# A selective scan that multiplies by C from SBUF: VectorE's products of two banks joined into one

## The chip, the cores and the metric

The kernel runs on one core of a Trainium2 chip. What is measured is the device time of one execution, in microseconds. Three runs of the kernel before took 8867.66, 8870.62 and 8871.87 us; their median, 8870.62, is the time before.

A core has five engines that work side by side and wait for each other through semaphores: PE (TensorE, matrix products into PSUM), ACT (ScalarE, functions and copies), DVE (VectorE), POOL (GpSimd) and SP, which issues DMA transfers. Each takes its instructions in a fixed order. SBUF and PSUM are the two memories on the chip[...].

## The reference

Four layers follow each other on four images of 64 x 64 tokens with 128 channels, all in fp32: a visual state-space block, an attention over all tokens of an image, a convolution block, and a neighbourhood attention with an MLP. The change lies in the first, whose core is a scan in four directions over the 4096 tokens of an image, with 256 channels (d) and 16 states (n) each:

```python
def step(h, t):
    x_t, d_t, B_t, C_t = t
    h = jnp.exp(d_t[..., None] * A) * h + (d_t * x_t)[..., None] * B_t[:, :, None, :]
    return (h, jnp.einsum('bkdn,bkn->bkd', h, C_t))
scan_in = (jnp.moveaxis(xs, -1, 0), jnp.moveaxis(delta, -1, 0), jnp.moveaxis(Bs, -1, 0), jnp.moveaxis(Cs, -1, 0))
h0 = jnp.zeros((Bn, K, DI, N), input.dtype)
_, ys_l = jax.lax.scan(step, h0, scan_in)
```

So for each channel and state: a factor exp(delta A), an input delta x B, the recurrence, a product with C, and a sum over the states.

## The kernel before

`network` (L1654 and below) first prepares image 0's scan inputs (`scan_inputs`: layer norm, projection, convolution, delta, and du = delta x) and then, at a lower urgency, emits the scans of all four images. Beside image 0's scan it emits the inputs of images 1 to 3, beside the scan of image `img` the remaining layers of image `img - 1` (`rest`), and after the last scan the remaining layers of image 3. A scheduler lays out each engine's instructions from priorities, so the scan's instructions and the other layers' are interleaved in each engine's fixed order.

`selective_scan` (L454 to L578) goes through four directions `k`, eight chunks of 512 tokens, two halves `hf` of the channels, four groups `j` of four states, and two pairs `pp`. One turn of the innermost loop is a *unit*: 128 partitions are 32 channels by 4 states, and two groups `g` of channels lie beside each other, so a unit is 128 x 2 x 512. There are 4 x 4 x 8 x 2 x 4 x 2 = 2048 units. Each does:

- POOL: `dB` = du x B, both in SBUF, 128 x 1024 (L501). `dB` has four tiles.
- ACT: `dA` = exp(delta A) into a PSUM bank, once for each `g` (L507). `dA` has three banks.
- DVE: the recurrence along 512 tokens, once for each `g` (L509), with dA, dB and the state that the chunk before left.
- the product with C, into a tile `hc`, by one of two engines. `ON_POOL` says by which, by the unit's number modulo 16: 5 of 16 units in image 0 and 7 of 16 in the others are POOL's, 832 in all; 1216 are VectorE's.
- PE: the sum over the states by a product with a matrix of zeros and ones, into `py` (L555).

In a unit whose product is POOL's, the scans write `hc` in SBUF, and POOL multiplies `hc` by `c_rows` in place, 128 x 1024 (L522); this instruction is put behind the dB of `BEHIND` = 2 later units. The last states of both `g` go to `state` in one copy by ACT (L518). In a unit whose product is VectorE's, a scan writes over `dA` in its PSUM bank, VectorE multiplies that bank by `c_rows` into a half of `hc` (L514, 128 x 512, once for each `g`), and ACT copies the last state out of the bank (L516), again once for each `g`. In all chunks but the last of a direction the state is kept.

A `dB` tile comes free when the unit's scans are done, a `dA` bank when its product and state copy are done. `Products` gives the `hc` tiles; `b_rows`, `c_rows`, `dt` and `du` come by DMA from DRAM, issued by SP.

`scan_inputs` has a tile `sz` for silu(z), 128 x 2 x 512, in a pool of two buffers (L351); ACT fills it (L359) and a DMA in ACT's queue stores it (L382) once for each of the 32 chunks. `scan_output` builds a small matrix `center` on VectorE from two SBUF tiles (L601), once for each image.

Of the kernel before, what the change touches and what calls it, by code (L numbers as in the profile page):

```python
# [28 lines left out]
F32 = mybir.dt.float32  # L29
# [10 lines left out]
ND = DI // 128  # L40
FF = 4 * C
NF = FF // 128
LC = 512
NCH = NT // LC
# [19 lines left out]
def bc(ap, shape):  # L64
    return ap.to_broadcast(list(shape))


def mid(ap, n):

    return bc(ap.unsqueeze(1), [ap.shape[0], n, ap.shape[1]])  # L70


def span(c, n=LC):
    return slice(c * n, (c + 1) * n)
# [103 lines left out]
def layernorm_T(tc, K, pool, psum, x, w, b, out):  # L178


    nc = tc.nc
    stats = pool.tile([128, 4, 6], F32, name="ln_stats", bufs=2)
    mv = pool.tile([128, 4, 2], F32, name="ln_mv", bufs=2)
    rstd = pool.tile([128, 4], F32, name="ln_rstd", bufs=2)
    less = pool.tile([128, 4], F32, name="ln_less", bufs=2)
    shift = pool.tile([128, 4], F32, name="ln_shift", bufs=2)
    for t in range(4):
        nc.vector.bn_stats(stats[:, t, :], x[:, t, :])
    for t in range(4):
        nc.vector.bn_aggr(mv[:, t, :], stats[:, t, :])  # L190
    rstd_of(nc, K, rstd, mv[:, :, 1])
    nc.scalar.activation(less, rstd, AF.Copy, scale=-1.0)
    for t in range(4):
        nc.scalar.activation(shift[:, t : t + 1], mv[:, t, 0:1], AF.Copy, scale=less[:, t : t + 1])
    xn = pool.tile([128, 4, 128], F32, name="ln_xn", bufs=1)
    pt = psum.tile([128, 4, 128], F32, name="ps")
    for t in range(4):
        nc.scalar.activation(  # L198
            xn[:, t, :], x[:, t, :], AF.Identity, bias=shift[:, t : t + 1], scale=rstd[:, t : t + 1]
        )  # L200
        nc.tensor.transpose(pt[:, t, :], xn[:, t, :], K.ident)  # L201
    nc.scalar.activation(out, pt.rearrange("p t c -> p (t c)"), AF.Identity, bias=b, scale=w)  # L202
# [37 lines left out]
def conv3x3(nc, out, lhsT, src, row0, nrows, height):  # L240


    taps = [(0, 0)] + [(dy, dx) for dy in (-1, 0, 1) for dx in (-1, 0, 1) if (dy, dx) != (0, 0)]
    for i, (dy, dx) in enumerate(taps):
        r0, r1 = max(row0, -dy), min(row0 + nrows, height - dy)
        c0, c1 = max(0, -dx), min(W, W - dx)
        mm = nc.tensor.matmul(  # L247
            out[:, r0 - row0 : r1 - row0, c0:c1],
            lhsT((dy + 1) * 3 + dx + 1),
            src[:, r0 + dy : r1 + dy, c0 + dx : c1 + dx],  # L250
            start=(i == 0),
            stop=(i == len(taps) - 1),
        )
    return mm


def token_tiles(dram, c):

    return dram[span(c), :].rearrange("(t p) c -> p t c", p=128)
# [17 lines left out]
def scan_inputs(tc, K, A, D, img):  # L277
# [4 lines left out]
    nc = tc.nc  # L282
    with ExitStack() as ctx:
        pool = ctx.enter_context(tc.tile_pool(name="si_a", bufs=2))
# [49 lines left out]
        for c in range(NCH + 1):  # L334
            acts = []
            if c < NCH:
                xt = pool.tile([128, 4, 128], F32, name="x")
                nc.sync.dma_start(xt, token_tiles(A["x"][img], c))
                xnT = pool.tile([128, LC], F32, name="xnT")
                layernorm_T(tc, K, pool, psum, xt, ln_w, ln_b, xnT)  # L340
                band = pool.tile([128, ND, RC + 2, W], F32, name="band", bufs=3)
                bands[c] = band
                for d in range(ND):
                    ps = psum.tile([128, LC], F32, name="ps")
                    nc.tensor.matmul(ps, in_proj[:, d * 128 : (d + 1) * 128], xnT, start=True, stop=True)
                    rows = ps.rearrange("p (h w) -> p h w", w=W)
                    nc.scalar.copy(band[:, d, 1 : RC + 1, :], rows)
                    if c > 0:
                        nc.scalar.copy(bands[c - 1][:, d, RC + 1, :], rows[:, 0, :])
                        nc.scalar.copy(band[:, d, 0, :], bands[c - 1][:, d, RC, :])  # L350
                sz = pool.tile([128, ND, LC], F32, name="sz")  # L351
                for d in range(ND):
                    ps = psum.tile([128, LC], F32, name="ps")
                    mm = nc.tensor.matmul(
                        ps, in_proj[:, DI + d * 128 : DI + (d + 1) * 128], xnT, start=True, stop=True
                    )
                    if d == 0:
                        together.open(mm)
                    acts.append(lambda d=d, ps=ps, sz=sz: nc.scalar.activation(sz[:, d, :], ps, AF.Silu))  # L359
            if c > 0:  # L360

                b, src = c - 1, bands.pop(c - 1)
                top, bottom = (1 if b == 0 else 0), (RC + 1 if b == NCH - 1 else RC + 2)
                for d in range(ND):
                    ps = psum.tile([128, LC], F32, name="ps")
                    mm = conv3x3(
                        nc,
                        ps.rearrange("p (h w) -> p h w", w=W),
                        lambda t, d=d: diag[:, d, t, :],
                        src[:, d, top:bottom, :],  # L370
                        1 - top,
                        RC,
                        bottom - top,
                    )
                    acts.append(
                        lambda d=d, ps=ps, b=b: nc.scalar.activation(
                            xc[:, d, span(b)], ps, AF.Silu, bias=conv_b[:, d : d + 1]
                        )
                    )
            together.run(mm, acts)  # L380
            if c < NCH:
                nc.scalar.dma_start(D.sz[img][c], sz)  # L382
            if c > 0:
                nc.scalar.dma_start(D.xc[img][c - 1], xc[:, :, span(c - 1)])
                steps(0, c - 1)
# [68 lines left out]
def selective_scan(tc, K, S, D, img):  # L454
# [8 lines left out]
    nc = tc.nc  # L463
    pool, psum, products = S.pool, S.psum, S.products
    waiting = []

    def settle(unit):
        while waiting and waiting[0][0] <= unit:
            waiting.pop(0)[1]()

    for k in ORDER:
        back = k >= 2
        order = slice(None, None, -1) if back else slice(None)
        last = 0 if back else LC - 1
        state = pool.tile([128, NJS, NPR, 2], F32, name="state")
        for i in range(NCH):
            c = NCH - 1 - i if back else i
            for hf in range(2):
# [11 lines left out]
                for j in range(NJS):  # L490

                    bt, ct = (pool.tile([128, LC], F32, name=name, bufs=4) for name in ("b_rows", "c_rows"))
# [4 lines left out]
                    hcs, made = [], []  # L497
                    for pp in range(2):
                        pr = 2 * hf + pp
                        dB = pool.tile([128, 2, LC], F32, name="dB", bufs=4)  # L500
                        nc.gpsimd.tensor_mul(dB, dus[pp], mid(bt, 2))  # L501
                        on_pool = S.unit % 16 in ON_POOL[img > 0]
                        S.unit += 1
                        hc = products.tile()
                        for g in range(2):
                            dA = psum.tile([128, LC], F32, name="dA", bufs=3)
                            nc.scalar.activation(dA, dts[pp][:, g, :], AF.Exp, scale=S.A[:, k, j, pr, g : g + 1])  # L507
                            hg = hc[:, g, :] if on_pool else dA
                            nc.vector.tensor_tensor_scan(  # L509
                                hg[:, order], dA[:, order], dB[:, g, order],  # L510
                                0.0 if i == 0 else state[:, j, pr, g : g + 1], ALU.mult, ALU.add,
                            )
                            if not on_pool:
                                mm = nc.vector.tensor_mul(hc[:, g, :], dA, ct)  # L514
                                if i < NCH - 1:
                                    nc.scalar.copy(state[:, j, pr, g : g + 1], dA[:, last : last + 1])  # L516
                        if on_pool and i < NCH - 1:
                            nc.scalar.copy(state[:, j, pr, :], hc[:, :, last])  # L518
                        if on_pool:

                            def product(hc=hc, ct=ct, made=made):
                                made.append(nc.gpsimd.tensor_mul(hc, hc, mid(ct, 2)))  # L522

                            waiting.append((S.unit + BEHIND, product))
                        else:
                            made.append(mm)
                        hcs.append(hc)
                        settle(S.unit)
# [1260 lines left out]
```

## Time and profile before

| what | value |
|---|---|
| median of three runs | 8870.62 us |
| the profiled execution's own time | 8860.92 us |
| its span | 8859.2 us |
| granted TensorE clock, mean | 0.861 |
| instructions | 102397 |
| units, with product on POOL / on VectorE | 832 / 1216 |

The last columns of a group's row in the profile are: busy time of the group in us, mean ns of one, then the idle time of its engine just before the instructions of the group, and what ended most of that. A group is named by its line, engine and operation, then what it writes, an arrow, and what it reads, by the names of the tiles. Instructions of an engine overlap at their ends, so two that follow each other take a little less than twice the length of one.

### The profile page before, as it was taken

The numbers are of one execution on the slowest core, as the hardware profiler recorded it, in microseconds if no ns is written. First come the engines' busy times: TensorE is split into PE (matmuls) and PEld (weight loads), VectorE is DVE, ScalarE is ACT, GpSimd is POOL, SyncE is SP. The second block draws the span as 40 slices with busy tenths as digits, with TensorE's granted clock in tenths as the row PEclk, the third lists the DMA queues.
The fourth block names the chain that finished last, engine by engine and source line by source line (L and its number), as shares of the span: only waits on it lengthen the run. The fifth ranks groups of instructions, "written<-read, shape, count | busy, mean of one in ns | idle before, by whom it ended". The sixth has DMA issues, their size and how long they took to land. (4 is left out here: it accounts for less than half of the span.)

```text
span 8859.2 us, 102397 instructions
## 1 busy us (share of the span) xinstructions
PE 7107.5 (80%) x30596; PEld 2643.4 (30%) x30596; DVE 7138.3 (81%) x8531; ACT 5683.3 (64%) x11661; POOL 7046.2 (80%) x3079
## 2 busy tenths in 40 slices
PE   6845858686788888887798988887899888888987
PEld 2211213132332222333322222333322223343333
DVE  4888978787999999998899999998899999313433
ACT  5646767676666676667766676667766766354365
POOL 6988999989899999998899989998899989300000
PEclk8756868687899998887899988888899988899989
DMA  5777776777555556666445556565445565220021
GB/s 183 246 233 247 244 254 233 265 241 257 188 169 168 173 166 218 193 214 194 164 167 173 175 187 216 193 218 182 159 165 180 179 211 194 77 70 4 1 82 30
DMA packets 863923, 1576.24 MB, mean 178 GB/s; under 512 B 218597, under 2 KB 345212, under 8 KB 859645
## 3 DMA queue, kind: packets, MB, share of 16 engines
q1 hardware_dynamic: 733053, 1393.40, 47.8%
q10 hardware_dynamic: 130304, 176.19, 5.6%
q8 instruction: 245, 4.01, 0.2%
q14 instruction: 321, 2.63, 0.1%
HBM read 1276.02 MB, written 282.28 MB: 176 GB/s over the span
## 5 line engine op out<-in xcount | busy, mean ns | idle before, releaser
L501 POOL TENSOR_TENSOR dB<-du,b_rows 128x1024 f32<-128x1024 f32 x2048 | 4808.9, 2378 | 451.2 <-issue 136.8
L507 ACT ACTIVATE dA<-dt,w_A_log 128x512 f32<-128x512 f32 x4096 | 2782.9, 691 | 482.0 <-DVE hc L509 213.5
L509 DVE TENSOR_TENSOR_SCAN dA<-dA,state,dB 128x512 f32<-128x512 f32 x2128 | 2630.0, 1272 | 277.1 <-POOL dB L501 138.8
L522 POOL TENSOR_TENSOR hc<-hc,c_rows 128x1024 f32<-128x1024 f32 x832 | 1979.2, 2379 | 54.3 <-issue 21.3
L509 DVE TENSOR_TENSOR_SCAN hc<-dA,state,dB 128x512 f32<-128x512 f32 x1456 | 1801.9, 1267 | 171.1 <-ACT dA L507 100.0
L514 DVE TENSOR_TENSOR hc<-dA,c_rows 128x512 f32<-128x512 f32 x2432 | 1564.6, 675 | 74.8 <-PE py L555 60.5
L555 PE MATMUL py<-hc,pick 128*32 128x512 f32 x8192 | 1254.7, 690 | 377.6 <-POOL hc L522 277.9
L516 ACT COPY state<-dA 128x1 f32<-128x1 f32 x2128 | 327.2, 159 | 1329.9 <-DVE hc L514 1320.7
L845 PE MATMUL pa<-e,l_v 128*128 128x512 f32 x2048 | 1056.5, 647 | 19.8 <-ACT e L801 19.7
L797 PE MATMUL pair<-l_g,l_f 32*128 32x512 f32 x2048 | 529.5, 665 | 176.7 <-ACT e L801 121.7
L985 POOL MEMSET l_h<- 64x128 f32 x8 | 1.7, 211 | 837.2 <-DVE l_h L959 834.9
L801 ACT ACTIVATE e<-pair 128x1024 f32<-128x1024 f32 (+1 forms) x448 | 508.3, 1135 | 219.2 <-PE pair L797 211.1
L845 PEld LDWEIGHTS pa<-e,l_v 128*128 128x128 f32 x2048 | 373.9, 199 | 672.1 <-issue 615.8
L555 PEld LDWEIGHTS py<-hc,pick 128*32 128x32 f32 x8192 | 209.2, 116 | 1156.8 <-issue 458.6
L247 PE MATMUL ps<-band,w_conv_diag 128*128 128x504 f32 (+3 forms) x1152 | 498.2, 592 | 6.1 <-ACT delta L397 5.7
L1317 PE MATMUL pair<-table,ident 128*128 128x512 f32 x768 | 404.4, 652 | 101.8 <-ACT e L1327 80.6
L509 DVE TENSOR_TENSOR_SCAN dA<-dA,dB 128x512 f32<-128x512 f32 x304 | 356.0, 1212 | 64.5 <-POOL dB L501 51.7
L1327 ACT ACTIVATE e<-pair 128x1024 f32<-128x1024 f32 (+1 forms) x224 | 254.9, 1138 | 192.6 <-PE pair L1321 192.0
L328 POOL TENSOR_TENSOR du<-delta,xc 128x1024 f32<-128x1024 f32 x128 | 332.9, 2607 | 52.2 <-ACT delta L397 46.7
L201 PE MATMUL ps<-ident,ln_xn 128*128 128x128 f32 x512 | 137.3, 367 | 257.8 <-ACT ln_xn L198 185.0
L219 PE MATMUL ps<-xnT,w_fc_w 128*128 128x512 f32 x512 | 270.2, 662 | 69.9 <-ACT xnT L202 29.2
L247 PEld LDWEIGHTS ps<-band,w_conv_diag 128*128 128x128 f32 x1152 | 220.4, 192 | 283.2 <-issue 262.5
(276 smaller groups left out, 8680.4 us busy)
## 6 DMA issues: line engine op xcount, KB each, us to landing
b_rows<-bc_dram SPq DMA_DIRECT2D x1024, 256.0 KB
c_rows<-bc_dram SPq DMA_DIRECT2D x1024, 256.0 KB
dt<-delta_dram SPq DMA_DIRECT2D x512, 512.0 KB
du<-du_dram SPq DMA_DIRECT2D x512, 512.0 KB
delta_dram<-delta ACTq DMA_DIRECT2D x128, 512.0 KB
du_dram<-du SPq DMA_DIRECT2D x128, 512.0 KB
table<-biasT_dram SPq DMA_DIRECT2D x72, 512.0 KB
y_first_dram<-y_sum ACTq DMA_DIRECT2D x128, 256.0 KB
```

Of the source, the lines that this page charges most:

```text
L247: mm = nc.tensor.matmul(out[:, r0 - row0 : r1 - row0, c0:c1], lhsT((dy + 1) * 3 + dx + 1), src[:, r0 + dy : r1 + dy, c0 + dx : c1 + dx], s ...
L328: nc.gpsimd.tensor_mul(du.rearrange("p d (a b) -> p d a b", b=H), deltas[b].rearrange("p d (a b) -> p d a b", b=H), tk,)
L501: nc.gpsimd.tensor_mul(dB, dus[pp], mid(bt, 2))
L507: nc.scalar.activation(dA, dts[pp][:, g, :], AF.Exp, scale=S.A[:, k, j, pr, g : g + 1])
L509: nc.vector.tensor_tensor_scan(hg[:, order], dA[:, order], dB[:, g, order], 0.0 if i == 0 else state[:, j, pr, g : g + 1], ALU.mult, ALU.add,)
L514: mm = nc.vector.tensor_mul(hc[:, g, :], dA, ct)
L522: made.append(nc.gpsimd.tensor_mul(hc, hc, mid(ct, 2)))
L555: mm = nc.tensor.matmul(py[0][32 * q : 32 * q + 32, :], S.pick, hcs[q // 2][:, q % 2, :], start=(k == 1 and j == 0), stop=(j == NJS - 1),)
L797: nc.tensor.matmul(ps[:, u, :], f[quad, t // 4, span(t % 4, 128)], g[quad, c, :], start=True, stop=True)
L801: made = nc.scalar.activation(e, ps, AF.Exp)
L845: nc.tensor.matmul(pa, v[:, 8 * q + t, :], es[q], start=(t == 0 and q == 0), stop=(t == 7 and q == 3),)
L1317: nc.tensor.matmul(ps[:, u, :], K.ident, t[:, u, :], start=True, stop=False)
```

## The change

In a unit whose product is VectorE's, the scan of each `g` now writes over its half of `dB` in SBUF, not over `dA` in PSUM. When both scans are done, one VectorE instruction multiplies all 1024 columns of `dB` by `c_rows` (taken twice) into `hc`, and ACT copies both last states in one instruction. The `dA` bank comes free with the scan; the `dB` tile comes free with the product and the state copy. `dB` has a fifth tile, and `sz` has one buffer instead of two. Units whose product is POOL's do what they did. The lines behind the change move up by two: POOL's product is L520, PE's sum L553, and both kinds of state copy are L516.

```diff
-                sz = pool.tile([128, ND, LC], F32, name="sz")
+                sz = pool.tile([128, ND, LC], F32, name="sz", bufs=1)
...
-                        dB = pool.tile([128, 2, LC], F32, name="dB", bufs=4)
+                        dB = pool.tile([128, 2, LC], F32, name="dB", bufs=5)
                         nc.gpsimd.tensor_mul(dB, dus[pp], mid(bt, 2))
...
                             nc.scalar.activation(dA, dts[pp][:, g, :], AF.Exp, scale=S.A[:, k, j, pr, g : g + 1])
-                            hg = hc[:, g, :] if on_pool else dA
+                            hg = (hc if on_pool else dB)[:, g, :]
                             nc.vector.tensor_tensor_scan(
                                 hg[:, order], dA[:, order], dB[:, g, order],
                                 0.0 if i == 0 else state[:, j, pr, g : g + 1], ALU.mult, ALU.add,
                             )
-                            if not on_pool:
-                                mm = nc.vector.tensor_mul(hc[:, g, :], dA, ct)
-                                if i < NCH - 1:
-                                    nc.scalar.copy(state[:, j, pr, g : g + 1], dA[:, last : last + 1])
-                        if on_pool and i < NCH - 1:
-                            nc.scalar.copy(state[:, j, pr, :], hc[:, :, last])
+                        if not on_pool:
+                            mm = nc.vector.tensor_mul(hc, dB, mid(ct, 2))
+                        if i < NCH - 1:
+                            nc.scalar.copy(state[:, j, pr, :], (hc if on_pool else dB)[:, :, last])
```

## Prediction

> **What bounds the kernel now.** I read the busy shares of the page first, then its slices, then one undisturbed stretch of the scan.
>
> ```profile
> PE 7107.5 (80%) x30596; PEld 2643.4 (30%) x30596; DVE 7138.3 (81%) x8531; ACT 5683.3 (64%) x11661; POOL 7046.2 (80%) x3079
> ...
> DVE  4888978787999999998899999998899999313433
> ...
> POOL 6988999989899999998899989998899989300000
> ```
>
> Three engines stand at about 80%, which says little. The slices say more: POOL works in eights and nines into slice 35 and then stops. That is the end of the scan; the last VectorE product of the timeline ends at 7618 us. So the span is 7618 us of scan, with other layers beside it, and 1241 us of the last image's later layers, which the change doesn't touch. In the table by stretch the line 2600 to 3200 holds scan and attention; its columns are the stretch, its length, and busy time (instructions) of PE, PEld, DVE, ACT, POOL, then clock, DMA share, GB/s.
>
> ```profile
> 2600.00:3200.00 600.00, 536.45 (x2210) 159.29 (x2210) 566.48 (x608) 398.25 (x753) 600.00 (x260) 0.95 0.52 171
> ```
>
> POOL is busy 600.00 of 600 us here: it is the bound, with DVE 5% behind. The groups give the prices.
>
> ```profile
> L501 POOL TENSOR_TENSOR dB<-du,b_rows 128x1024 f32<-128x1024 f32 x2048 | 4808.9, 2378 | 451.2 <-issue 136.8
> L509 DVE TENSOR_TENSOR_SCAN dA<-dA,state,dB 128x512 f32<-128x512 f32 x2128 | 2630.0, 1272 | 277.1 <-POOL dB L501 138.8
> L514 DVE TENSOR_TENSOR hc<-dA,c_rows 128x512 f32<-128x512 f32 x2432 | 1564.6, 675 | 74.8 <-PE py L555 60.5
> L854 DVE TENSOR_TENSOR total<-total,e 128x2048 f32<-128x2048 f32 x56 | 128.3, 2292 | 136.9 <-ACT e L801 136.8
> L601 DVE TENSOR_TENSOR center<-center,ident 128x128 f32<-128x128 f32 x4 | 15.9, 3984 | 0.1
> ```
>
> The last row is the one to stop at. L601 adds two 128x128 tiles that both lie in SBUF; its four durations are 11.21, 0.28, 4.15 and 0.29 us. The two short ones ran while POOL did nothing. The timeline (start, length, engine) shows what the long ones had beside them:
>
> ```profile
> 2214.86 6.93 POOL L501 TENSOR_TENSOR dB<-du,b_rows 128x1024 f32<-128x1024 f32 x3
> 2215.32 11.21 DVE L601 TENSOR_TENSOR center<-center,ident 128x128 f32<-128x128 f32 x1
> 2221.76 2.33 POOL L522 TENSOR_TENSOR hc<-hc,c_rows 128x1024 f32<-128x1024 f32 x1
> 2224.05 2.33 POOL L501 TENSOR_TENSOR dB<-du,b_rows 128x1024 f32<-128x1024 f32 x1
> 2226.46 2.32 DVE L509 TENSOR_TENSOR_SCAN hc<-dA,dB 128x512 f32<-128x512 f32 x2
> ...
> 5908.52 2.39 POOL L522 TENSOR_TENSOR hc<-hc,c_rows 128x1024 f32<-128x1024 f32 x1
> 5909.20 4.15 DVE L601 TENSOR_TENSOR center<-center,ident 128x128 f32<-128x128 f32 x1
> 5910.82 2.39 POOL L501 TENSOR_TENSOR dB<-du,b_rows 128x1024 f32<-128x1024 f32 x1
> ```
>
> Both ended within 0.15 us of the moment when POOL ran out of work (2226.38, 5913.21), after five POOL instructions in the one case and two in the other. VectorE did not get in between two POOL instructions that followed each other.
>
> **What the skill says.** "SBUF — State Buffer", section "Who interferes with whom": a VectorE instruction with two SBUF inputs takes its second through the read port that it shares with GpSimd, and contends with a GpSimd instruction that reads SBUF; one with at most one SBUF input does not. The trace agrees: L514 now has dA in PSUM, and its longest is 0.71 us beside a busy POOL, as the scans' is 1.32. The page has the loser wait for one instruction; L601 waited for two and five, and the measurement decides. "GPSIMD Engine Reference", section "Instruction dispatch": a core goes on to the next Pool instruction as soon as its own share is done. The trace agrees: three L501 take 6.95 us, 2.32 each, less than one's 2.36, so there is no gap to slip into. "VectorE: DVE Perf Modes", section "The perf-mode tier table": fp32 tensor_tensor makes one result per cycle wherever its inputs lie, so moving dA out of PSUM brings no faster mode; L854 shows it, 2048 columns in 2292 ns.
>
> **The change, part by part.** Of 2048 units 832 multiply on POOL (P units: 5 of 16 in image 0, 7 of 16 later), 1216 on VectorE (V units).
>
> (a) *Two products become one.* A pair of L514 takes 1.27 us in the timeline. One of 1024 columns from two SBUF tiles, between L601's free 0.28 at 128 columns and L854's 2.29 at 2048: 0.28 + 896 x 1.048 ns = 1.22 us. It saves 0.05 us each, 61 us of VectorE in all.
>
> (b) *The product now reads dB and c_rows, both in SBUF, beside a POOL that reads SBUF in every multiply.* This is the part that decides. By L601 the product starts when POOL has run dry. Behind it on VectorE stand the next unit's scans; for those POOL waits in turn, since they free dB tiles and give its P product. I follow one stretch from the end of a product, which frees a tile. P unit then V unit: POOL makes a dB (0.1 to 2.4), VectorE scans P (to 2.44), which frees the next tile and the P product, so POOL goes on with a dB and a product to 0.1 + 3 x 2.32 = 7.1. VectorE has scanned V by 4.88 and stands 2.2 us. Then 1.22: the pair takes 8.3. A V unit that follows a V unit: scans 2.44, in which POOL makes its one dB and goes idle, then 1.22: 3.7.
> Images 1 to 3: 16 units are 7 such pairs and 2 single V: 7 x 8.3 + 2 x 3.7 = 65.5 us; 32 such groups, three images: 6288. Image 0: 5 pairs and 6 singles, 63.7 x 32 = 2038, and 128 du products (L328) of 2.61: 334; 2372. Sum 8660 us.
> Onto it come POOL's idle times that have nothing to do with VectorE's scans. It was idle 7618 - 7046 = 572 us in the scan; waits for L509 were 91 + 78 = 169 of these and are already in the walk. 403 stay: 9063 us.
> A second way, over VectorE: busy in the scan 7138 - 365 (after 7620 us) = 6773; less 61; 832 pairs x 2.2 = 1830 of standing; its idle time of before, 845, less 267 for POOL's dB: 578. Sum 9120. The two agree to 1%.
>
> (c) *V scans write dB in SBUF instead of dA in PSUM.* The P scans do that already: 1267 against 1272 ns. Nothing. A dB tile is held longer, until product and state copy are done; the fifth tile meets that, and (b) counts tiles as freed by the product. A dA bank comes free after the scan, so the exponentials run ahead. VectorE waited 125 + 119 us for those; I count no gain, because POOL and the port set the pace now.
>
> (d) *One state copy of two columns instead of two of one.* 1064 copies at 0.19 for 2128 at 0.16: 137 us less of ACT, which is 64% busy. Before, ACT stood 1321 us at L516 for VectorE (releaser L514), with the next exponentials queued behind it; the copy now waits for the second scan instead, ahead of the product. That lies beside other work, since ACT sets no pace: VectorE's waits for exponentials under (c) are all that it cost.
>
> (e) *sz with one buffer.* The next chunk's Silu waits for one store. 32 chunks lie in the first 2212 us (L328's last start), some 69 us apart, so the store is long done; nothing, and at worst a few us at each of 31.
>
> Sum: 9063 + 1241 + 1.7 outside the span = 10306, against this execution's own 8860.9 (span 8859.2). The median of the runs is 9.7 above that: 10310 us, +16%.
>
> **The rivals.**
> *Fair turns.* The product gets in after one POOL instruction, as the page words it, and POOL then waits. For it: VectorE's small tensor-scalars at L1213 and L1215 ended at such boundaries, after 2.38 us each. Against it: L601. POOL's 7046 and 1216 x 1.22 = 1484 cannot overlap, so 8530, with some 150 to 400 of idle time: 8.7 to 8.9 ms of scan, about 10050.
> *Longer starving.* A single V also meets a POOL with a queue, and stands one instruction more: 384 singles x 2.32 = 890 us at most; half of it gives 10750. For it: five tiles let POOL run on, and 11.21 us at L601. Against: while VectorE stands no tile comes free, so POOL soon runs dry.
> *No contention for this form: not slower.* The gain is then what POOL waited for VectorE, at most 169 us; half of it gives 8785. It decides if the unit's products show 1.22 us beside a running POOL. For it: both the state and other small SBUF operands are read today without a stall. Against it: two long L601 out of two beside POOL.
>
> **How the numbers follow.** Forecast 0.63, fair turns 0.20, longer starving 0.10, no contention 0.07. The forecast's own spread is the 403 us of old waits, which may all vanish beside the new ones or come twice, and the pair's 8.3 us; with fair turns below and half of the starving case above, the range is 9850 to 10700. Measurement of this kernel tells about 0.2% from no change. Faster 0.06, within 0.2% 0.01, slower 0.93.
>
> **What would show it.** L514 as hc<-dB,c_rows 128x1024, x1216, with a mean near 1.22 + 1830 / 1216 = 2.7 us, shortest 1.2, longest above 4; POOL's multiplies still 2.36 long (fair turns would lengthen those that wait for the port), but POOL idle with L514 as releaser, in sum over 1500 us; POOL in no stretch at 100%; scan end near 9060; the tail 1241 as before. A mean of 1.2 to 1.3 for L514 proves the forecast wrong. So would a scan end past 9600, where VectorE waits behind more than one queue of POOL.

## The result, and the profile after

The changed kernel takes 10154.72 us in the median of six runs (10143.32 to 10165.12), against 8872.08 us in six runs of the kernel before on the same chip. The ratio is 1.1448, with a 95% interval of 1.1436 to 1.1461: 14.5% slower. The forecast was 10310 us, 1.5% too high; the range held the time.

The page of the changed kernel, its first two parts and the groups that answer to those of before:

```profile
PE 7489.2 (74%) x30596; PEld 2759.8 (27%) x30596; DVE 8526.9 (84%) x7315; ACT 5596.3 (55%) x10597; POOL 7827.2 (77%) x3079
...
DVE  5889989888799999999999999999999999502433
...
POOL 6987999989889998998899998998889987500000
...
L501 POOL TENSOR_TENSOR dB<-du,b_rows 128x1024 f32<-128x1024 f32 x2048 | 5027.8, 2467 | 829.4 <-DVE hc L514 409.2
...
L514 DVE TENSOR_TENSOR hc<-dB,c_rows 128x1024 f32<-128x1024 f32 x1216 | 2915.3, 2400 | 146.4 <-PE py L553 61.5
...
L520 POOL TENSOR_TENSOR hc<-hc,c_rows 128x1024 f32<-128x1024 f32 x832 | 2438.6, 2931 | 64.6 <-issue 24.1
...
L328 POOL TENSOR_TENSOR du<-delta,xc 128x1024 f32<-128x1024 f32 x128 | 385.4, 3016 | 47.0 <-ACT delta L397 45.1
```

Two groups of POOL as they were before:

```profile
L522 POOL TENSOR_TENSOR hc<-hc,c_rows 128x1024 f32<-128x1024 f32 x832 | 1979.2, 2379 | 54.3 <-issue 21.3 <-ACT state L518 20.5 <-PE py L555 4.0
L328 POOL TENSOR_TENSOR du<-delta,xc 128x1024 f32<-128x1024 f32 x128 | 332.9, 2607 | 52.2 <-ACT delta L397 46.7 <-DMA du_dram<-du 3.5 <-ACT state L518 1.9
```

VectorE has fewer instructions (7315 for 8531) and is busy for longer. One product of 1024 columns lasts 2400 ns in the mean. POOL has the same 3079 instructions, and they have grown: by 219 us at L501, 459 at L520 (2931 ns for 2379) and 53 at L328, 731 us in all. VectorE's slices are now a row of nines. So both engines stand inside their instructions, in time that the profile counts as busy. For POOL there is a listed wait as well, 409.2 us before dB (L501) for the product (hc L514).

How they stand is seen in the timeline of the changed kernel, in a stretch where the pattern repeats (start, length, engine):

```profile
3220.25 4.64 POOL L501 TENSOR_TENSOR dB<-du,b_rows 128x1024 f32<-128x1024 f32 x2
3220.37 2.43 DVE L509 TENSOR_TENSOR_SCAN dB<-dA,state,dB 128x512 f32<-128x512 f32 x2
3222.89 3.08 DVE L514 TENSOR_TENSOR hc<-dB,c_rows 128x1024 f32<-128x1024 f32 x1
3224.86 3.33 POOL L520 TENSOR_TENSOR hc<-hc,c_rows 128x1024 f32<-128x1024 f32 x1
3225.90 2.44 DVE L509 TENSOR_TENSOR_SCAN hc<-dA,state,dB 128x512 f32<-128x512 f32 x2
3228.14 4.65 POOL L501 TENSOR_TENSOR dB<-du,b_rows 128x1024 f32<-128x1024 f32 x2
3228.27 2.43 DVE L509 TENSOR_TENSOR_SCAN dB<-dA,state,dB 128x512 f32<-128x512 f32 x2
3230.79 3.09 DVE L514 TENSOR_TENSOR hc<-dB,c_rows 128x1024 f32<-128x1024 f32 x1
```

The product is ready at 3222.89, while POOL makes a dB until about 3224.9. It runs then, for 1.1 us, although POOL has the next multiply at hand: L520 starts at 3224.86 and lasts 3.33 us instead of 2.36, since it waits for the product to end. VectorE stood 1.9 us, POOL 1.0. A pair of units takes 3230.79 - 3222.89 = 7.90 us. Of all 1216 products, 1204 let no second POOL instruction go ahead of them. And the wait of POOL is no single case: 723 of its 2880 multiplies at L501 and L520 last longer than 2.6 us, where before none of the 2880 did.

The span splits like this; the first number is the start of the last scan in the timeline, the second what is left of the span:

| | last scan | after it | span |
|---|---|---|---|
| before | 7616 | 1243 | 8859.2 |
| after | 8778 | 1381 | 10159.1 |
| difference | +1162 | +138 | +1300 |

The second part was not expected to change. The table by stretch has more work in it, first before, then after:

```profile
7618.00:8859.00 1241.00, 1052.99 (x5202) 477.39 (x5194) 366.46 (x587) 609.99 (x921) 0.79 (x4) 0.92 0.12 38
```

```profile
8780.00:10159.00 1379.00, 1149.85 (x5787) 520.45 (x5775) 373.57 (x610) 641.88 (x974) 0.80 (x4) 0.91 0.11 35
```

PE has 5787 matmuls there instead of 5202. The blocks of the last layer's attention, counted by the VectorE instruction that writes oT, number 14 there instead of 11; an image has 8. So before, 3 of image 2's stood behind the scan together with image 3's 8, and now 6 do: work that had lain beside the scan has moved behind it.

The mean granted TensorE clock is lower too (0.817 for 0.861). That explains little of the longer scan: of VectorE's idle time up to the last scan, 105 us ended with PE (90 before), of POOL's 9 (69 before).

### The profile page after: what moved, and what is told of

Same layout as the page of the kernel before. It is cut to its first block, busy times and chain, and to the rows that moved or that the text cites. A ratio compares the mean times of both kernels' runs of the same rounds, so it can differ in the third digit from the quotient of the medians.

```text
span 10159.1 us, 100683 instructions
## 1 busy us (share of the span) xinstructions
PE 7489.2 (74%) x30596; PEld 2759.8 (27%) x30596; DVE 8526.9 (84%) x7315; ACT 5596.3 (55%) x10597; POOL 7827.2 (77%) x3079
## 5 line engine op out<-in xcount | busy, mean ns | idle before, releaser
L501 POOL TENSOR_TENSOR dB<-du,b_rows 128x1024 f32<-128x1024 f32 x2048 | 5027.8, 2467 | 829.4 <-DVE hc L514 409.2
L514 DVE TENSOR_TENSOR hc<-dB,c_rows 128x1024 f32<-128x1024 f32 x1216 | 2915.3, 2400 | 146.4 <-PE py L553 61.5
L509 DVE TENSOR_TENSOR_SCAN dB<-dA,state,dB 128x512 f32<-128x512 f32 x2128 | 2603.4, 1258 | 176.7 <-ACT dA L507 139.7
L520 POOL TENSOR_TENSOR hc<-hc,c_rows 128x1024 f32<-128x1024 f32 x832 | 2438.6, 2931 | 64.6 <-issue 24.1
L553 PE MATMUL py<-hc,pick 128*32 128x512 f32 x8192 | 1275.1, 703 | 341.1 <-POOL hc L520 219.4
L843 PE MATMUL pa<-e,l_v 128*128 128x512 f32 x2048 | 1151.6, 698 | 46.4 <-ACT e L799 44.4
L553 PEld LDWEIGHTS py<-hc,pick 128*32 128x32 f32 x8192 | 219.0, 119 | 1154.0 <-issue 590.8
L516 ACT COPY state<-dB 128x2 f32<-128x2 f32 x1064 | 202.5, 190 | 414.6 <-DVE dB L509 359.5
L328 POOL TENSOR_TENSOR du<-delta,xc 128x1024 f32<-128x1024 f32 x128 | 385.4, 3016 | 47.0 <-ACT delta L397 45.1
L509 DVE TENSOR_TENSOR_SCAN dB<-dA,dB 128x512 f32<-128x512 f32 x304 | 353.6, 1198 | 27.9 <-ACT dA L507 20.4
L305 PE MATMUL ps<-xc,w_x_proj_w 128*128 128x512 f32 x256 | 223.7, 1016 | 178.8 <-ACT xc L376 127.9
L795 PEld LDWEIGHTS pair<-l_g,l_f 32*128 32x128 f32 x2048 | 148.7, 200 | 739.2 <-ACT e L799 484.4
```

The source lines that it names most:

```text
L328: nc.gpsimd.tensor_mul(du.rearrange("p d (a b) -> p d a b", b=H), deltas[b].rearrange("p d (a b) -> p d a b", b=H), tk,)
L509: nc.vector.tensor_tensor_scan(hg[:, order], dA[:, order], dB[:, g, order], 0.0 if i == 0 else state[:, j, pr, g : g + 1], ALU.mult, ALU.add,)
L514: mm = nc.vector.tensor_mul(hc, dB, mid(ct, 2))
L553: mm = nc.tensor.matmul(py[0][32 * q : 32 * q + 32, :], S.pick, hcs[q // 2][:, q % 2, :], start=(k == 1 and j == 0), stop=(j == NJS - 1),)
L795: nc.tensor.matmul(ps[:, u, :], f[quad, t // 4, span(t % 4, 128)], g[quad, c, :], start=True, stop=True)
L843: nc.tensor.matmul(pa, v[:, 8 * q + t, :], es[q], start=(t == 0 and q == 0), stop=(t == 7 and q == 3),)
```

## The experiments

The theory from these lines: product and POOL take turns at a port that both need, one instruction each. Rivals: the product gets in only when POOL has run dry (the forecast's), and causes that have no port in them: the later release of dB, the tile counts, the planner's order (the planner is the scheduler that lays out each engine's instructions). The diffs show the lines that matter, most of them in `selective_scan`; `last scan` and `rest` below are as in the table.

**e1: the tile counts alone.** The kernel before, with five dB tiles and one sz buffer.

```diff
-                sz = pool.tile([128, ND, LC], F32, name="sz")
+                sz = pool.tile([128, ND, LC], F32, name="sz", bufs=1)
...
-                        dB = pool.tile([128, 2, LC], F32, name="dB", bufs=4)
+                        dB = pool.tile([128, 2, LC], F32, name="dB", bufs=5)
```

> The kernel before with only the change's tile counts: five dB tiles instead of four and one sz buffer; scans still write dA in PSUM, two products and two state copies per V unit. If the product's second SBUF input is the cost, nothing of it is here: 8800 to 8880 us, a small gain at most from POOL's 169 us of waits for the scans. If one sz buffer or the later release of tiles were part of the loss, this run is slower than before by more than 0.5%.

8970.33 us, ratio 1.0126 (1.0109 to 1.0143): 1.3% slower, against the expectation. Last scan 7642, rest 1317. Of the 100 us in the span, 74 lie behind the scan:

```profile
7643.00:8959.00 1316.00, 1106.72 (x5558) 501.92 (x5558) 371.80 (x602) 628.39 (x950) 1.78 (x5) 0.92 0.11 36
```

5558 matmuls are left over after the scan, where before 5202 were. No product and no port has changed here. The tile counts change the order that the planner lays out, and that leaves more of image 2's attention for the end (13 blocks, for 11 before).

**e6: one sz buffer alone.**

> The kernel before with one sz buffer instead of two and nothing else. If the loss of the run with both tile counts (1.26%) comes from the Silu that waits for the store of sz, this run is slower than before by about 1% and shows ACT or DVE waiting in the first 2300 us. If it comes from the fifth dB tile and the order that the planner makes with it, this run is within 0.3% of before.

8860.84 us, ratio 0.9992 (0.9985 to 0.9999), rest 1238. The single sz buffer costs nothing. What e1 lost came with the fifth dB tile, by elimination: no run has five dB tiles and two sz buffers.

**e2: the second input from PSUM.** The kernel after, with one operand exchanged.

```diff
-                            mm = nc.vector.tensor_mul(hc, dB, mid(ct, 2))
+                            mm = nc.vector.tensor_mul(hc, dB, mid(dA, 2))
```

> The kernel after, but the one 1024-column product takes as its second input the PSUM bank dA of the second group, read twice, instead of c_rows in SBUF. It leaves the product with C out of VectorE's units. Instruction count, shape, dB held until the product, and the joint state copy stay. Port theory: the product takes 1.2 to 1.3 us everywhere, POOL's products are 2.36 again, and the time is 8700 to 8900 us. Rival, that the later release of dB or the in-place scan in SBUF costs the time: 9900 to 10200 us, as after.

8933.48 us, ratio 1.0075 (1.0058 to 1.0092). Last scan 7593, rest 1335. The groups of this kernel:

```profile
L514 DVE TENSOR_TENSOR hc<-dB,dA 128x1024 f32<-128x1024 f32 x1216 | 1479.5, 1218 | 227.3 <-PE py L553 139.8
...
L501 POOL TENSOR_TENSOR dB<-du,b_rows 128x1024 f32<-128x1024 f32 x2048 | 4805.3, 2377 | 425.2 <-DVE hc L514 148.5
L520 POOL TENSOR_TENSOR hc<-hc,c_rows 128x1024 f32<-128x1024 f32 x832 | 1978.2, 2378 | 40.7 <-ACT state L516 16.0
```

Here every product takes 1.22 us (the longest too), and POOL's multiplies are back at 2.38. The same instruction, held tile, scan in SBUF and joint copy, without the second SBUF operand: the scan ends 1185 us earlier than in the changed kernel. That is 0.97 us for each of 1216 products: the second SBUF operand is the cost, and POOL's shorter multiplies show whom it meets. (One thing more differs: the bank of the second `g` is now held until the product. If that does anything, it holds back the next exponential, so it does not explain the gain.) Against before, the scan is 22 us shorter and the rest 91 us longer.

**e11: the same with four dB tiles** (`bufs=4`).

> The kernel with the second input in PSUM (it leaves the product with C out of VectorE's units) and four dB tiles instead of five. The port is out of play, so it shows what the rest of the change is worth without the fifth tile. If the fifth tile and the planner's order with it cost what they cost on the kernel before (about 100 us), 8800 to 8850; a joint product and an earlier dA bank then gain at most 0.5%, because POOL is the bound. If the later release of dB hurts with four tiles, 8950 to 9100.

8901.45 us, ratio 1.0036 (1.0022 to 1.0051), between the two expectations. Last scan 7577, rest 1324. Without the port the rest of the change shortens the scan by 39 us, and what is left over for the end takes 80 back. As in e2, one of the unit's two dA banks is held longer than in the changed kernel, so the gain from an earlier dA bank is measured only in part.

**e8: the kernel after with four dB tiles** (`bufs=4`).

> The kernel after with four dB tiles as before (and one sz buffer). Turns at the port: a dB tile is held for the whole of a product that waits, so POOL runs dry sooner; it then lets VectorE in at once but loses its lead. I expect the two to cancel to within 2%: 10100 to 10350 us. Dry-POOL theory (my forecast's): a shorter run of POOL ahead of VectorE makes the waits shorter, 9900 to 10150.

10059.03 us, ratio 1.1346 (1.1327 to 1.1365): a little below what I expected of turns, and inside what the forecast's theory gives, so it does not part the two. Last scan 8698, rest 1354. The fifth tile is no help: without it the kernel is about 1% faster.

**e3: the product in two halves.**

```diff
-                            mm = nc.vector.tensor_mul(hc, dB, mid(ct, 2))
+                            for q in range(2):
+                                mm = nc.vector.tensor_mul(hc[:, q, :], dB[:, q, :], ct)
```

> The kernel after with its product cut into two of 512 columns, both inputs in SBUF. If POOL and VectorE take turns at the port instruction by instruction, POOL's waiting multiply gets in between the halves, and the second half waits a whole multiply more: up to 1216 x 2.3 = 2800 us more on VectorE, of which a part was idle time of POOL: 10800 to 12000 us, and a first half near 1.7 us, a second near 2.5. If VectorE keeps the port while it has work for it, only the 1216 x 0.06 us of the extra instruction come on top: 10200 to 10300 us. If VectorE gets in only when POOL is dry, as I had forecast, both halves run together and the time is also 10200 to 10300, but POOL's multiplies are not lengthened.

10542.54 us, ratio 1.1894 (1.1874 to 1.1913). The timeline:

```profile
3311.97 2.43 DVE L509 TENSOR_TENSOR_SCAN dB<-dA,state,dB 128x512 f32<-128x512 f32 x2
3314.32 3.50 DVE L515 TENSOR_TENSOR hc<-dB,c_rows 128x512 f32<-128x512 f32 x2
3314.48 2.79 POOL L521 TENSOR_TENSOR hc<-hc,c_rows 128x1024 f32<-128x1024 f32 x1
```

The first half runs, POOL's waiting multiply runs next (2.79 us with its wait), then the second half: two halves last 3.50 us. Over all units the first half has a median of 0.77 us and the second 2.82. POOL gets in between two VectorE instructions that have no gap between them. That is turns, and neither of the other two cases. The time is below the 10800 that I had for turns: VectorE is busy for 3642 us with the halves, only 727 more than with the whole products, and POOL's busy time falls by 325 us to 7502, since it waits less inside its own multiplies.

**e4: the product in eight pieces of 128 columns.**

```diff
-                            mm = nc.vector.tensor_mul(hc, dB, mid(ct, 2))
+                            for q in range(8):
+                                part = span(q % 4, 128)
+                                mm = nc.vector.tensor_mul(hc[:, q // 4, part], dB[:, q // 4, part], ct[:, part])
```

> The kernel after with its product cut into eight of 128 columns, the width of the small addition (L601) that had waited through five POOL instructions. Turns: the pieces cost 8 x 0.2 = 1.6 us for 1.16, and POOL gets in between pieces whenever it has work, so a product lasts as long as POOL has work: 11500 to 14000 us, no piece waits for more than one POOL instruction. If a narrow instruction is the one that starves, single pieces wait through two or more POOL instructions, with lengths of 4 to 11 us, as L601 had.

11223.40 us, ratio 1.2664 (1.2639 to 1.2690), below the range for turns. The medians of the pieces are 0.37, 2.43, then 0.28 us six times: POOL takes one turn, mostly between the first and the second piece, and then mostly stands for a dB tile (1185 us of idle time before L501 that ended with the pieces). Only 1 of 9728 pieces waited through two POOL instructions. So width alone is not what made L601 wait so long.

**e5 and e10: a small addition in each V unit.** The kernel before, with an addition like L601's into a tile that nothing reads (e5), and with a fill in front of it and tied behind the unit's product (e10, whose lines are shown; the tile's set-up is left out).

```diff
...
+                            after(tc, nc.vector.memset(K.scrap, 0.0), mm, mybir.DependencyClass.NoSync)
+                            nc.vector.tensor_add(K.scrap, K.scrap, K.ident)
                             made.append(mm)
```

> The kernel before, with one more VectorE instruction in each V unit: an addition of two 128x128 SBUF tiles in place, into a tile that nothing reads; a copy in kind of the L601 that waited through five POOL instructions. Turns: each addition waits for the rest of one POOL instruction, 0 to 2.35 us, about 1.2 us in the mean if they meet at random, and costs 0.2 us itself; VectorE's load grows by up to 1216 x 1.4 = 1700 us of which its 5% of idle time takes a part: 9400 to 10400 us, single additions at 0.28 to 2.7 us. If this kind (narrow, in place) starves behind a POOL that has work, many additions last 4 to 11 us and the time is above 10500.

> The kernel before with two more VectorE instructions in each V unit, spread over the whole scan and tied behind the unit's product: a fill of a 128x128 tile, as stands in front of L601, and the addition of two 128x128 SBUF tiles in place. It asks what made L601 wait through up to seven POOL instructions in the kernels measured so far. If a narrow in-place addition behind a fill starves while POOL has work, hundreds of the 1216 additions last 4 to 16 us and the time is above 10200. If it takes turns as the product does, none lasts over 3 us, the mean is near 0.3 + 1.1 = 1.4 us, and the time is 9500 to 10100: L601 then is an exception that this doesn't explain.

e5 reached its aim only in part: 9328.80 us (ratio 1.0521, 1.0500 to 1.0542), with its additions all drawn into the first 1500 us by the planner, many beside an idle POOL (median 0.29 us). Still 281 of them waited, none over 2.91 us. e10 has them spread over the scan: 9736.35 us, ratio 1.0977 (1.0955 to 1.0999).

```profile
L529 DVE TENSOR_TENSOR scrap<-scrap,ident 128x128 f32<-128x128 f32 x1216 | 1307.3, 1075 | 14.7
```

1.08 us in the mean; one of the 1216 took 5.76, the next longest 2.98. The 5.76 waited through two POOL instructions. A copy in kind of L601 takes turns too, if there is one in each V unit. In the same kernel the four instances of `center` itself, 11.21 us at most before, took 2.09 at most.

**e12: rare pairs.** This pointed to what had happened lately at the port. The kernel before, with an addition in each 32nd V unit (L532) and one in the V unit behind it (L534). The set-up of the counter and the tiles is left out.

```diff
...
+                            S.vunit += 1
+                            if S.vunit % 32 == 0:
+                                after(tc, nc.vector.tensor_add(K.scrap, K.scrap, K.ident), mm, mybir.DependencyClass.NoSync)
+                            if S.vunit % 32 == 1:
+                                after(tc, nc.vector.tensor_add(K.scrap2, K.scrap2, K.ident), mm, mybir.DependencyClass.NoSync)
```

> The kernel before with 38 pairs of small in-place additions of two SBUF tiles (128x128, into tiles that nothing reads), a pair in two V units that follow each other, then 30 V units with none. It asks whether turns are taken only after the port has lately changed hands: L601, which waited through up to six POOL instructions, is the first such instruction in hundreds of microseconds, while in the kernels with an addition or a product in each V unit only 3 of some 3600 waited through two, two of these three just after a POOL instruction on a part of the partitions. If a pause is what matters, the first of a pair often lasts 4 to 16 us and the second at most 3. If both stay under 3 us, the pause is not it, and L601 stays unexplained. The time tells little: 8870 to 9100 us.

The rows by line, with shortest, median and longest in ns:

```profile
L532 DVE TENSOR_TENSOR scrap<-scrap,ident x38: 280/7865/16526, 295.0 to 7764.9; 128x128 f32<-128x128 f32 x38
```

```profile
L534 DVE TENSOR_TENSOR scrap<-scrap,ident x38: 276/1482/2167, 109.1 to 7583.1; 128x128 f32<-128x128 f32 x38
```

The first of a pair has a median of 7.9 us; 22 of 38 let one to six POOL instructions start ahead of them. The second has a median of 1.5 us, the longest 2.2, and not one lets another go first, though in 25 cases POOL had its next multiply at hand. (There are 37 pairs: the very first addition at L534 and the last at L532 have no partner.) Same instruction, same tiles in kind, 1 to 13 us apart. So L601 was a true sample, of another case.

What makes the case is not the pause at the port alone. All first additions come after the same pause of some 30 V units (other layers' VectorE instructions not counted), and 35 met a running POOL. The 22 that let others go met a POOL that had at least 15 instructions behind it without a gap (less than 0.06 us from one to the next), up to 91; each of them got in only when POOL ran dry. The other 13 met one with at most 11, and in 8 of these POOL had its next multiply at hand and the addition got in first all the same. And since a first addition that waits leaves POOL dry, the second one always meets a short run, 14 at most. So e12 does not part a pause of VectorE's claims from a long unbroken run of POOL; its own firsts speak for the run. One `center` addition in e11 speaks against it as a strict rule: it got in after 0.50 us, behind 228 instructions without a gap.

The 76 additions sum to 273 us of VectorE's time; the kernel took 8992.94 us against 8861.46, one run each.

**e9: one unit less for POOL.** The kernel before, with 6 of 16 POOL products in images 1 to 3.

```diff
-ON_POOL = ((1, 4, 7, 10, 13), (0, 2, 4, 6, 9, 11, 13))
+ON_POOL = ((1, 4, 7, 10, 13), (0, 3, 6, 8, 11, 13))
```

> The kernel before with 6 instead of 7 of 16 units multiplied by POOL in images 1 to 3. POOL is the bound of the undisturbed stretches (600.00 of 600 us) with VectorE at 94%: one unit in 16 moved takes 2.32 of 53.4 us off POOL and puts 1.2 on VectorE's 50. If POOL's time is what counts, 8650 to 8800 us; if the two engines' waits for each other count as much, no change within 0.5%. No VectorE instruction with two SBUF inputs is added, since V products read a PSUM bank.

9005.48 us, ratio 1.0160 (1.0144 to 1.0177): 1.6% slower, and neither of the two expectations. But the scan is 62 us shorter (last scan 7553) and the rest 205 us longer (1449):

```profile
7554.00:9001.00 1447.00, 1209.87 (x6122) 547.46 (x6120) 377.32 (x622) 660.98 (x1002) 0.80 (x4) 0.91 0.10 34
```

6122 matmuls left over, for 5202. POOL lost 96 products, 236 us at L522, and the scan only 62: in the stretch 2600 to 3200 VectorE is now busy for 593 us and POOL for 596, so the two are level and moving work between them gains little. And a faster scan is no gain while other layers' work is then laid behind it. None of the versions beats the kernel before by more than e6's 0.1%.

## Why the prediction was right, step by step

*What bounds it, and what the change does to it: right.* POOL set the pace with VectorE close behind, the change puts a second SBUF operand into VectorE's product, and that collides with POOL at the port. e2 takes the operand away and with it 1185 us of the scan. "SBUF — State Buffer", section "Who interferes with whom", says so; the runs agree, to the PSUM operand that is free of it.

*(a) The product's own length: right.* 1.22 us forecast, 1218 ns in e2.

*(b) How it waits: wrong in its rule, and its standing too large.* The walk, the stretch that (b) of the prediction follows, had the product wait until POOL ran dry. The runs show turns (e3, 1204 of 1216 products, and 723 lengthened multiplies of POOL). The rival "fair turns" was the right one in this: its scan of 8.7 to 8.9 ms holds the measured 8.78, and its total of 10050 us is nearer than the forecast's. The mistake was to take L601 for a rule. It met a POOL that had 17 and 227 instructions without a gap behind it, the case that e12 shows, where the product comes every few microseconds; and L1213 and L1215, which the prediction names and sets aside, had shown the other case. The lock that "SBUF — State Buffer", section "Who interferes with whom", describes, held for a whole instruction while the other engine waits, is what the products show.
The wrong rule shows in the parts. The walk had 2.2 us of standing at each of 832 products behind a P unit and none at the 384 behind a V unit. In the order that VectorE ran, 797 products follow the scans of a P unit and 419 those of a V unit, and both last 2.40 us in the mean: 1.18 us of standing each, about half of the one figure and far more than the other. In sum VectorE stood 2915.3 - 1216 x 1.218 = 1434 us, for 1830. The prediction's second sum, over VectorE up to the last scan, shows that this is the term that was mis-sized (measured figures rounded):

| VectorE, us | forecast | measured |
|---|---|---|
| its own work | 6712 | 6718 |
| standing inside the product | 1830 | 1434 |
| idle | 578 | 627 |
| sum | 9120 | 8778 |

That the sum was no further off has a reason and some luck: under either rule POOL and the product exclude each other, and the two errors of the walk go opposite ways. POOL's multiplies at 2.36 and its 1500 us of waits for L514 were wrong: they are 731 us longer, and 409 us are waits for L514. The mean length was 2.40 us, for 2.7; the longest 5.66, as forecast above 4.

*The old idle time of POOL, 403 us on top: near.* In the changed kernel POOL is idle for 952 us up to the last scan; less 409 for the product and 66 for the scans, 477 are left. The old waits did not vanish beside the new ones.

*(c) Scans into SBUF at no cost, and the fifth tile to meet the later release:* right in the first: the scans are no slower (1258 ns for 1272). The fifth tile was not needed; e8 is faster without it.

*(d) and (e): right in what they count for.* ACT is busy 87 us less, for the 137 forecast; what that alone is worth, no run shows. One sz buffer costs nothing (e6).

*The rest behind the scan, 1241 us "as before": wrong, by 138 us.* Here the prediction had no step at all. It took the order of the other layers for given, while the planner lays it out anew for each change of tiles or units: 1317 us in e1, 1324 in e11, 1335 in e2, 1449 in e9, none of which has a two-SBUF product. That the planner expects a shorter scan and so places less beside it would fit all four; it was argued and not tested. The errors of +285 us (9063 for 8778) and -138 us are of opposite sign; that the total is within 1.5% is luck in this part. (The forecast's own sum comes to 10316 us; it was put down as 10310.)

*Rival "longer starving":* fell as it was put, for only 12 of 1216 products let a further POOL instruction go. That the singles stand too was right, for 1.18 us each; the rival had 2.32 at most.

*Rival "no contention":* fell; the products show 2.40 us and not 1.22. With the port out of play (e2, e11) the scan is only 22 and 39 us shorter and the kernel as a whole no faster, so the parts of the change that these two runs keep had little to win.

## What to carry to other kernels

Before moving an operand from PSUM to SBUF, count the SBUF inputs of the VectorE instruction. With two of them it and GpSimd's multiplies shut each other out here, and since GpSimd set the pace, each product of 1.22 us cost 0.97 us of the scan, times 1216. A lone long instance of an instruction is a sample of its own circumstances; before it prices a thousand others, ask whether they come as it came. And where a planner fills a long stage with other layers' work, look behind the stage too: one more dB tile moved 74 us there.

## What the hardware showed that I had not expected

Who goes first at the port is not always a matter of turns. In e12 the first addition after some 30 V units without one waited 7.9 us in the median and up to 16.5, through as many as six POOL instructions; the addition in the next V unit 1.5 us, never more than 2.2. In that trace a VectorE instruction was passed over only where POOL had run 15 or more instructions without a gap, and never where it had run 14 or fewer, whatever the pause before. Whether the run or the pause decides, and what in the hardware does it, stays open. Two of the few long waits in kernels with steady claims came just behind a POOL instruction that covers only a part of the partitions (5.66 us behind a 64-partition fill in the changed kernel, 5.76 us behind a one-partition multiply in e10), which would fit with cores of GpSimd that run apart from each other until a gap or a lost turn brings them together again. That is a guess; no run tests it.
